# Attention over lists of neighbours: scores and values of two heads by one 128x128 weight load, with zeros beside the queries

## The chip, the cores and the metric

The kernel runs on one core of a Trainium2 chip. The time is the device time of one execution in microseconds (us). The kernel before takes 2416.37 us, the median of three timed runs (2408.73 to 2416.6). The profile is of a further execution, which took 2205.58 us. A core has five engines with queues of their own: TensorE (PE; its weight loads are shown as PEld), VectorE (DVE), ScalarE (ACT), GpSimd (POOL) and SyncE (SP), which here only issues transfers. TensorE writes into PSUM; the other data lie in SBUF, with 128 partitions each.

## The reference

One layer for 4096 tokens of width 512: attention with a mask, and then a mixture of 8 experts of which each token uses 2.

```python
adj = jnp.maximum(adjacency_matrix, eye)
q = jnp.einsum('nd,hdk->hnk', node_matrix, Wqs)        # 8 heads of 64
k = jnp.einsum('nd,hdk->hnk', node_matrix, Wks)
v = jnp.einsum('nd,hdk->hnk', node_matrix, Wvs)
scores = jnp.einsum('hqk,hmk->hqm', q, k) * kd ** (-0.5)
scores = scores + IDENTITY_BIAS * eye - MASK_VAL * (1.0 - adj)
att = jax.nn.softmax(scores, axis=-1)
return jnp.einsum('hqm,hmk,hko->qo', att, v, Wo)
...
x = x + attention(layernorm(x), adj)
x = x + experts(layernorm(x))      # top 2 of 8, exact gelu, hidden width 512
```

All is in float32. The adjacency is random and thin: most pairs of tokens are masked.

## The kernel before

The kernel has three stages. In the first it normalizes, projects queries, keys and values, writes them to DRAM and finds, for each block of 128 queries, the list of keys that any of its queries sees. In the second it does the attention over these lists. In the third it runs the experts. The change touches only the second stage.

The work of that stage is a row of items. A block of 128 queries has one item for its own 128 keys (the diagonal, `c = -1`) and one for each 128 keys of its list, `LISTED` of them, 363 in all. A list is sorted so that its first items hold keys that only the first 64 queries see and its last ones keys that only the last 64 see; such a half item is computed for 64 queries, the others for 128. By the constants, 134 of the 363 are for 128 queries, beside the 32 diagonal ones.

```python
FIRST_ALONE = [10, 6, 5, 5, 4, ...]      # items of the first half alone
SECOND_FROM = [25, 14, 12, 10, 10, ...]  # from here, of the second half alone
...
def load_q(i):                            # P = 128, NP = 4 pairs of heads, KD = 64
    q_in[i] = qp.tile([P, NP, P], F32, tag="q", name=f"q_{i}")
    nc.sync.dma_start(out=q_in[i], in_=qT_d[:, :, ts(i, P)])
```

For each item the keys and values are gathered by GpSimd, nine items ahead. Then TensorE turns the keys around, multiplies keys by queries, and multiplies values by the exponentials, all with the two heads of a pair in two halves of the array:

```python
def turn(n):
    kT[n] = work.tile([P, NP, P], F32, tag="kT", bufs=3, ...)
    pk = ps_k.tile([P, 2, TB], F32, tag="k", ...)
    for p in range(NP):
        for r in range(2):
            half = slice(r * KD, (r + 1) * KD)
            nc.tensor.transpose(pk[:, r, ts(p, KD)], kv[n][half, ts(p, P)], ident[half, half])
    nc.scalar.copy(kT[n].rearrange(...), pk[...].rearrange(...))

def scores(n):
    ...
    for p in range(NP):
        for r in range(2):
            rows = slice(r * KD, (r + 1) * KD)
            nc.tensor.matmul(part(s[r], i, c)[:, p, :], k[rows, p, :], q_in[i][rows, p, q],
                             start=True, stop=True)
    ...
    for r in range(2):
        nc.scalar.activation(e[:, r * NP : (r + 1) * NP], part(s[r], i, c), AF.Exp)

def masked(n):                            # e = e * mask, on VectorE
    ...

def values(n):
    ...
    for p in range(NP):
        for r in range(2):
            h = 2 * p + r
            nc.tensor.matmul(
                po[i][r * KD : (r + 1) * KD, p, q], v[:, ts(h, KD)], e[:, r * NP + p, :],
                start=(c < 0 and p == 0), stop=(c == listed[i] - 1), ...)
    if c >= 0:
        nc.vector.tensor_add(acc[i][:, :, q], acc[i][:, :, q], e)
```

In a product the operand that comes second is the one that is loaded into the array (128 columns of keys, or 64 columns of values), and the third one streams through it, one column for each query.

The loop runs the three steps of different items side by side. After a block's last item its sums, its output projection and the gates of the experts follow in pieces, one for each later item:

```python
for n, (i, c) in enumerate(items):
    ...                                   # fetch(n + 9), load_q, load_x
    if c < 0 and i:
        osb[i - 1] = single.tile([P, NP, P], F32, tag="o", bufs=2, ...)
        nc.scalar.copy(osb[i - 1], po.pop(i - 1))
    if n + 3 < len(items):
        turn(n + 3)
    if n + 2 < len(items):
        scores(n + 2)
    values(n)
    later(n)                              # a piece of the block before
    if n + 2 < len(items):
        masked(n + 2)
```

Of the kernel before, what the change touches and what calls it, by code (L numbers as in the profile page):

```python
# [20 lines left out]
P = 128  # L21
# [22 lines left out]
def kernel(  # L44
# [172 lines left out]
    waiting = []  # L217

    def load_q(i):
        q_in[i] = qp.tile([P, NP, P], F32, tag="q", name=f"q_{i}")  # L220
        nc.sync.dma_start(out=q_in[i], in_=qT_d[:, :, ts(i, P)])

    def gather(to, src, of, i, c):

# [43 lines left out]
    with tc.tile_pool(name="wqkv", bufs=1) as wp, tc.tile_pool(name="p1", bufs=3) as work, tc.tile_pool(  # L268
# [355 lines left out]
        for u in range(8 * NTB + 1):  # L624
            b, s = divmod(u, 8)
            if u in load_at:
                load_adj(load_at[u])
            due = []
            for k in range(8):
                if u - k in lists_from:  # L630
                    due += lists_at(lists_from[u - k], k)
            nxt = (b + 1) * TPB
            if b < NTB:
                if b + 1 < NTB:
                    if s < 4:
                        tokens_1(nxt + s)
                    else:
                        tokens_2(nxt + s - 4)
                        if b + 2 < NTB:
                            load_x1(nxt + TPB + s - 4)  # L640
                if s < 4:
                    project_kv(b, s)
                else:
                    if s == 4:
                        qT = block.tile([P, NP, TB], F32, tag="qT", name=f"qT_{b}")
                    project_q(b, s - 4, qT)
                    if s == 7:
                        nc.sync.dma_start(out=qT_d[:, :, ts(b, TB)], in_=qT)
                if b + 1 < NTB and s >= 4:
                    tokens_3(nxt + s - 4)  # L650
            if u - 2 in load_at:
                neighbours(load_at[u - 2])
                if load_at[u - 2] == NT - 1:

                    ap_cm.__exit__(None, None, None)
                    kv_cm = tc.tile_pool(name="kv", bufs=AHEAD + 1, side="right")
                    kvp = kv_cm.__enter__()
                    q_cm = tc.tile_pool(name="q", bufs=2, side="right")
                    qp = q_cm.__enter__()
                    load_q(0)  # L660
                    fetch(0)
            if u == 8 * NTB - 4:
                for n in range(1, AHEAD):
                    fetch(n)
            for f in due:
                f()
            if u - 8 in lists_from:
                g = lists_from[u - 8]
                ready += [
                    (i, c) for i in range(g * G, g * G + G) for c in range(listed[i])  # L670
                    if c % 5 in (1, 3)
                ]
            if u < 8 * NTB - 4:
                for _ in range(min(3, len(ready))):
                    pack()
# [26 lines left out]
    def route_1(m, l, pool, name):  # L702


        own = l.unsqueeze(3).to_broadcast([P, m, E, E])
        other = l.unsqueeze(2).to_broadcast([P, m, E, E])
        ahead = pool.tile([P, m, E, E], F32, tag="ahead", name=f"ahead_{name}")
        nc.vector.tensor_tensor(ahead, other, own, op=ALU.is_gt)
        same = pool.tile([P, m, E, E], F32, tag="same", name=f"same_{name}")
        nc.vector.tensor_tensor(same, other, own, op=ALU.is_equal)  # L710
        nc.vector.tensor_mul(same, same, before.unsqueeze(1).to_broadcast([P, m, E, E]))
        nc.vector.tensor_add(ahead, ahead, same)
        rank = pool.tile([P, m, E], F32, tag="rank", name=f"rank_{name}")
        nc.vector.tensor_reduce(rank, ahead, axis=AX.X, op=ALU.add)
        chosen = pool.tile([P, m, E], BF16, tag="chosen", name=f"chosen_{name}")
        nc.vector.tensor_single_scalar(chosen, rank, 2.0, op=ALU.is_lt)
        counts = pool.tile([P, m, E], BF16, tag="counts", name=f"counts_{name}")
        nc.vector.tensor_copy(counts, count.unsqueeze(1).to_broadcast([P, m, E]))
        if m > 1:
            more = pool.tile([P, E], F32, tag="chosen_m", name=f"chosen_m_{name}")  # L720
            nc.vector.tensor_reduce(
                more, chosen.rearrange("p m e -> p e m"), axis=AX.X, op=ALU.add
            )
            nc.vector.tensor_add(count, count, more)
        else:
            nc.vector.tensor_add(count, count, chosen[:, 0])
        return rank, chosen, counts
# [115 lines left out]
    with tc.tile_pool(name="p2a", bufs=2) as two, tc.tile_pool(  # L843
# [36 lines left out]
                group_of[i] = len(groups) - 1  # L880

        def load_x(i):
            x_in[i] = two.tile([P, D], F32, tag="xt", name=f"xr_{i}")
            nc.sync.dma_start(out=x_in[i], in_=x[ts(i, P), :])

        def turn(n):
            kT[n] = work.tile([P, NP, P], F32, tag="kT", bufs=3, name=f"kT_{n}")

            pk = ps_k.tile([P, 2, TB], F32, tag="k", name=f"pk_{n}")
            for p in range(NP):  # L890
                for r in range(2):
                    half = slice(r * KD, (r + 1) * KD)
                    nc.tensor.transpose(  # L893
                        pk[:, r, ts(p, KD)], kv[n][half, ts(p, P)], ident[half, half]
                    )
            nc.scalar.copy(  # L896
                kT[n].rearrange("k p (r j) -> k r p j", r=2),
                pk[:, :, : NP * KD].rearrange("k r (p j) -> k r p j", p=NP),
            )

        def queries(i, c):
            h = half_of(i, c)
            return slice(0, P) if h is None else ts(h, QH)

        def part(t, i, c):

            if half_of(i, c) is None:
                return t
            heads = t.shape[1]
            t = t.rearrange("p h q -> p (h q)")[:, : heads * QH]  # L910
            return t.rearrange("p (h q) -> p h q", h=heads)

        def scores(n):

            i, c = items[n]
            s = [ps_s.tile([P, NP, P], F32, tag="s", name=f"s{r}_{i}_{c}") for r in range(2)]
            k = kT.pop(n)
            q = queries(i, c)
            for p in range(NP):
                for r in range(2):  # L920
                    rows = slice(r * KD, (r + 1) * KD)
                    nc.tensor.matmul(  # L922
                        part(s[r], i, c)[:, p, :], k[rows, p, :], q_in[i][rows, p, q],
                        start=True, stop=True,
                    )
            if c < 0:
                e = two.tile([P, 2 * NP, P], F32, tag="acc", name=f"acc_{i}")
                acc[i] = e
            else:
                e = part(work.tile([P, 2 * NP, P], F32, tag="e", name=f"e_{i}_{c}"), i, c)  # L930
            for r in range(2):
                nc.scalar.activation(e[:, r * NP : (r + 1) * NP], part(s[r], i, c), AF.Exp)  # L932
            es[n] = e

        def masked(n):
# [7 lines left out]
        def values(n):  # L943
            i, c = items[n]
            e = es.pop(n)
            if c < 0:
                po[i] = ps_o.tile([P, NP, P], F32, tag="o", name=f"po_{i}")
            v = kv.pop(n)[:, H * KD :]
            q = queries(i, c)
            for p in range(NP):  # L950
                for r in range(2):
                    h = 2 * p + r

                    nc.tensor.matmul(  # L954
                        po[i][r * KD : (r + 1) * KD, p, q], v[:, ts(h, KD)], e[:, r * NP + p, :],
                        start=(c < 0 and p == 0), stop=(c == listed[i] - 1),
                        skip_group_check=True,
                    )
            if c >= 0:
                nc.vector.tensor_add(acc[i][:, :, q], acc[i][:, :, q], e)  # L960

# [3 lines left out]
        LAST = 6  # L965
        jobs = []
        first_of_step = []

        def piece(i, k):
            g = group_of[i]  # L970
# [2 lines left out]
            if k == 1:  # L973
                sums[i] = ps_e.tile([P, P], F32, tag="e", name=f"sums_{i}")
                a = acc.pop(i)
                for t in range(2):
                    for q in range(4):
                        u, r = divmod(q, 2)
                        nc.tensor.matmul(
                            sums[i][q * Q4 : (q + 1) * Q4], half_q[:, t],  # L980
                            a[:, r * NP + 2 * u + t, :], start=(t == 0), stop=(t == 1),
                            tile_position=(0, q * Q4), skip_group_check=True,
                        )
            if k == 2:
# [119 lines left out]
        for n, (i, c) in enumerate(items):  # L1104
# [2 lines left out]
                fetch(n + AHEAD)  # L1107
            if c == 2 and i + 1 < NT:
                load_q(i + 1)
            if c == 2:  # L1110
                load_x(i)
            if n >= 56 and n % 7 == 0 and loads:
                e, d = loads.pop(0)
                nc.sync.dma_start(out=w1[:, e, d], in_=W1[e, ts(d, P), :])
            if c < 0 and i:
                osb[i - 1] = single.tile([P, NP, P], F32, tag="o", bufs=2, name=f"o_{i - 1}")
                nc.scalar.copy(osb[i - 1], po.pop(i - 1))
            if n + 3 < len(items):
                turn(n + 3)
            if n + 2 < len(items):  # L1120
# [4 lines left out]
                masked(n + 2)  # L1125
            if c == listed[i] - 1:
                left.append((n, i))
        osb[NT - 1] = single.tile([P, NP, P], F32, tag="o", bufs=2, name=f"o_{NT - 1}")
        nc.scalar.copy(osb[NT - 1], po.pop(NT - 1))

        work_cm.__exit__(None, None, None)
        q_cm.__exit__(None, None, None)
# [286 lines left out]
```

## Time and profile before

| | us |
|---|---|
| timed, median of 3 | 2416.37 |
| profiled execution | 2205.58 |
| span of its trace | 2203.7 |
| attention stage, about | 510 to 1590 |
| experts, about | 1630 to 2190 |

The costliest groups of the page that belong to the stage of the change follow. A row names line, engine, operation, output and inputs, the shape in the array (rows*columns) and of the tile, and the count; after the first bar stand the busy time and the mean of one in ns, after the second the idle time of the engine before them and what ended it. In TensorE's groups the mean is longer than the busy time divided by the count, as instructions overlap.

```profile
L922 PE MATMUL s<-q,kT 64*128 64x64 f32 (+1 forms) x5808 | 409.4, 282 | 2.7 <-ACT acc L932 2.7
L922 PEld LDWEIGHTS s<-q,kT 64*128 64x128 f32 x5808 | 373.4, 196 | 2.9 <-ACT acc L932 2.9
L954 PE MATMUL po<-e,kv 128*64 128x64 f32 (+1 forms) x5808 | 311.3, 251 | 0.0
L954 PEld LDWEIGHTS po<-e,kv 128*64 128x64 f32 x5808 | 246.4, 141 | 34.7 <-issue 0.8
L893 PE MATMUL pk<-ident,kv 64*128 64x64 f32 x2904 | 172.4, 240 | 11.4 <-ACT kT L896 11.0
```

L893 is the transpose of the keys, L922 the scores, L954 the values. The 5808 of L922 are 363 listed items by 8 products by 2 instructions; a float32 product is two instructions, a transpose is one. The diagonal items stand in smaller groups of their own.

### The profile page before, as it was taken

Reading aid. Unit: us, or ns where it says so; the run is one execution under the profiler, and the core shown is the slowest. Engines: PE = TensorE matmul, PEld = TensorE weight load, DVE = VectorE, ACT = ScalarE, POOL = GpSimd, SP = SyncE. Lnnn points to the kernel's source line nnn. Section 1 sums busy time; section 2 is a strip of 40 time slices with the busy share of each in tenths; the row PEclk is TensorE's granted clock in tenths of the full one; section 3 lists DMA queues with packets and bytes.
Section 4 is the critical chain, followed back from the end, with each engine's and each line's share of the span. In section 5 each row is a group of like instructions: output and inputs, shape, how many; then the busy total and the mean of one; then the engine's idle time right before and its main releaser. Section 6 shows DMA issues by size and latency. Waiting matters only on the chain. (4 is left out here: it accounts for less than half of the span.)

```text
span 2203.7 us, 52479 instructions
## 1 busy us (share of the span) xinstructions
PE 2040.5 (93%) x20620; PEld 1366.7 (62%) x20620; DVE 1319.2 (60%) x2387; ACT 870.1 (39%) x1842; POOL 1242.8 (56%) x1072
## 2 busy tenths in 40 slices
PE   7877879899999999999999999999829999999998
PEld 3333334348888888888788878777614444444444
DVE  4888586724887767777677777777723222333232
ACT  2121211124666646655556555656412222222222
POOL 1769888885888657678676766667412112111112
PEclk9988988896999989999999999999959999999999
DMA  7737787847788868878788878878475556555554
GB/s 281 301 127 234 258 294 261 263 120 236 247 260 273 273 216 275 281 239 282 247 268 266 267 249 248 264 234 252 165 257 127 134 131 136 136 134 140 137 136 96
DMA packets 215039, 481.71 MB, mean 219 GB/s; under 512 B 49618, under 2 KB 81874, under 8 KB 210692
## 3 DMA queue, kind: packets, MB, share of 16 engines
q0 software_dynamic: 79232, 242.18, 37.1%
q1 hardware_dynamic: 134404, 234.01, 33.7%
q8 instruction: 168, 2.75, 0.5%
q10 hardware_dynamic: 1152, 2.10, 0.3%
q14 instruction: 83, 0.68, 0.1%
HBM read 400.59 MB, written 77.58 MB: 217 GB/s over the span
## 5 line engine op out<-in xcount | busy, mean ns | idle before, releaser
L225 POOL DMA_INDIRECT kv<-kv_d,key_of x363 | 430.4, 1186 | 231.8 <-PE po L954 136.4
L941 DVE TENSOR_TENSOR e<-e,mask 128x512 f32<-128x512 f32 (+1 forms) x363 | 322.6, 889 | 204.0 <-ACT e L932 200.4
L922 PE MATMUL s<-q,kT 64*128 64x64 f32 (+1 forms) x5808 | 409.4, 282 | 2.7 <-ACT acc L932 2.7
L1354 POOL DMA_INDIRECT out_dram<-y,r x71 | 110.6, 1558 | 474.0 <-ACT h L1324 124.7
L922 PEld LDWEIGHTS s<-q,kT 64*128 64x128 f32 x5808 | 373.4, 196 | 2.9 <-ACT acc L932 2.9
L896 ACT COPY kT<-pk 128x512 f32<-128x512 f32 x395 | 232.1, 588 | 285.1 <-PE pk L893 277.3
L932 ACT ACTIVATE e<-s 128x256 f32<-128x256 f32 (+1 forms) x726 | 297.1, 461 | 101.5 <-PE s L922 98.6
L960 DVE TENSOR_TENSOR acc<-acc,e 128x512 f32<-128x512 f32 (+1 forms) x363 | 320.4, 883 | 1.4 <-PE po L954 1.4
L954 PE MATMUL po<-e,kv 128*64 128x64 f32 (+1 forms) x5808 | 311.3, 251 | 0.0
L225 POOL DMA_INDIRECT mask<-in_adjT_dram,mask_of x230 | 257.7, 1121 | 71.9 <-issue 50.0
L457 POOL TENSOR_SCALAR started<-slots,base 128x384 bf16<-128x384 int16 (+12 forms) x96 | 229.0, 2401 | 76.6 <-DVE longer L407 75.7
L954 PEld LDWEIGHTS po<-e,kv 128*64 128x64 f32 x5808 | 246.4, 141 | 34.7 <-issue 0.8
L1318 PE MATMUL ph<-w,xT 128*128 x568 | 258.3, 598 | 0.7 <-ACT xT L207 0.7
L1347 PE MATMUL py<-w,hT 128*128 x568 | 255.6, 593 | 0.9 <-DVE hT L1332 0.9
L352 DVE TENSOR_REDUCE flags<-adjT 128x64 f32<-128x4096 f32 x32 | 141.2, 4413 | 81.2 <-DMA adjT<-in_adjT_dram 81.2
L1352 DVE TENSOR_TENSOR y<-py,bb 128x512 f32<-128x512 f32 x71 | 49.1, 692 | 225.6 <-PE py L1347 184.2
L893 PE MATMUL pk<-ident,kv 64*128 64x64 f32 x2904 | 172.4, 240 | 11.4 <-ACT kT L896 11.0
L893 PEld LDWEIGHTS pk<-ident,kv 64*128 64x128 f32 x2904 | 122.0, 142 | 77.0 <-issue 47.2
L1318 PEld LDWEIGHTS ph<-w,xT 128*128 128x128 f32 x568 | 103.2, 192 | 104.1 <-issue 103.0
L1347 PEld LDWEIGHTS py<-w,hT 128*128 128x128 f32 x568 | 102.5, 190 | 104.0 <-issue 102.8
L225 POOL DMA_INDIRECT pm<-in_adjT_dram,mask_of x133 | 130.5, 981 | 41.5 <-issue 33.6
L1353 ACT ACTIVATE y<-y,gate 128x512 f32<-128x512 f32 x71 | 51.2, 722 | 213.1 <-DVE y L1352 213.1
(589 smaller groups left out, 2405.3 us busy)
## 6 DMA issues: line engine op xcount, KB each, us to landing
adjT<-in_adjT_dram SPq DMA_DIRECT2D x32, 2048.0 KB
bb<-in_L_ffn_b_dram SPq DMA_DIRECT2D x142, 256.0 KB
r<-xs_d SPq DMA_DIRECT2D x71, 258.0 KB
kv_d<-kv SPq DMA_DIRECT2D x32, 512.0 KB
xt<-in_x_dram SPq DMA_DIRECT2D x32, 256.0 KB
qT_d<-qT SPq DMA_DIRECT2D x8, 1024.0 KB
q<-qT_d SPq DMA_DIRECT2D x32, 256.0 KB
xr<-in_x_dram SPq DMA_DIRECT2D x32, 256.0 KB
```

What stands on the lines that cost most here:

```text
L225: nc.gpsimd.indirect_dma_start(out=to, out_offset=None, in_=src, in_offset=bass.IndirectOffsetOnAxis(ap=of[:, at[i] + c : at[i] + c + 1], ...
L352: nc.vector.tensor_reduce(flags[g][:, :, j, :], adj_in.pop(i).rearrange("p c (h q) -> p h c q", h=2), axis=AX.X, op=ALU.max,)
L457: nc.gpsimd.tensor_scalar(started[i, k], slots[:, t0 * P : t1 * P], base[g][:, k, j : j + 1], None, op0=ALU.is_ge,)
L893: nc.tensor.transpose(pk[:, r, ts(p, KD)], kv[n][half, ts(p, P)], ident[half, half])
L896: nc.scalar.copy(kT[n].rearrange("k p (r j) -> k r p j", r=2), pk[:, :, : NP * KD].rearrange("k r (p j) -> k r p j", p=NP),)
L922: nc.tensor.matmul(part(s[r], i, c)[:, p, :], k[rows, p, :], q_in[i][rows, p, q], start=True, stop=True,)
L932: nc.scalar.activation(e[:, r * NP : (r + 1) * NP], part(s[r], i, c), AF.Exp)
L941: nc.vector.tensor_mul(e, e, m.unsqueeze(1).to_broadcast(e.shape))
L954: nc.tensor.matmul(po[i][r * KD : (r + 1) * KD, p, q], v[:, ts(h, KD)], e[:, r * NP + p, :], start=(c < 0 and p == 0), stop=(c == listed[i ...
L960: nc.vector.tensor_add(acc[i][:, :, q], acc[i][:, :, q], e)
L1318: nc.tensor.matmul(ph, xTs[b][:, c, :], w1[:, bass.ds(es[b], 1), c, :], start=(c == 0), stop=(c == DC - 1),)
L1347: nc.tensor.matmul(py, hTs[b][:, c, :], w2[:, bass.ds(es[b], 1), c, :], start=(c == 0), stop=(c == HC - 1),)
```

## The change

The two heads of a pair are no longer put into two halves of the array. One load of 128 x 128 holds the keys (or the values) of both heads. For the scores, the queries of the two heads stand side by side, 256 columns in place of 128, and each has zeros in the rows of the other head, so that a column of the product holds the scores of one head alone. For the values both heads' exponentials stream through both heads' values; of the product's four quarters the two with a head's own values are kept, and the other two are left in PSUM unused. The aim is one weight load where there were two, and no products in parts of the array.

```diff
     def load_q(i):
-        q_in[i] = qp.tile([P, NP, P], F32, tag="q", name=f"q_{i}")
-        nc.sync.dma_start(out=q_in[i], in_=qT_d[:, :, ts(i, P)])
+        q_in[i] = q_two[i % 2]
+        for r in range(2):
+            rows = slice(r * KD, (r + 1) * KD)
+            nc.sync.dma_start(out=q_in[i][rows, :, r, :], in_=qT_d[rows, :, ts(i, P)])
...
+                    q_two = [qp.tile([P, NP, 2, P], F32, name=f"q_{k}") for k in range(2)]
+                    for t in q_two:
+                        for r in range(2):
+                            rows = slice(r * KD, (r + 1) * KD)
+                            nc.gpsimd.memset(t[rows, :, 1 - r, :], 0.0)
...
         def turn(n):
-            pk = ps_k.tile([P, 2, TB], F32, tag="k", name=f"pk_{n}")
+            pk = ps_k.tile([P, NP, P], F32, tag="k", name=f"pk_{n}")
             for p in range(NP):
-                for r in range(2):
-                    half = slice(r * KD, (r + 1) * KD)
-                    nc.tensor.transpose(
-                        pk[:, r, ts(p, KD)], kv[n][half, ts(p, P)], ident[half, half]
-                    )
-            nc.scalar.copy(kT[n].rearrange(...), pk[...].rearrange(...))
+                nc.tensor.transpose(pk[:, p, :], kv[n][:, ts(p, P)], ident)
+            nc.scalar.copy(kT[n], pk)
...
         def scores(n):
-            s = [ps_s.tile([P, NP, P], F32, tag="s", name=f"s{r}_{i}_{c}") for r in range(2)]
             for p in range(NP):
-                for r in range(2):
-                    rows = slice(r * KD, (r + 1) * KD)
-                    nc.tensor.matmul(
-                        part(s[r], i, c)[:, p, :], k[rows, p, :], q_in[i][rows, p, q],
-                        start=True, stop=True,
-                    )
+                if p == 0 or full and p == NP // 2:
+                    s.append(ps_s.tile(
+                        [P, NP // 2, 2, P] if full else [P, NP, 2, QH], F32, tag="s",
+                        name=f"s{p}_{i}_{c}",
+                    ))
+                nc.tensor.matmul(
+                    s[-1][:, p - (len(s) - 1) * NP // 2], k[:, p, :], q_in[i][:, p, :, q],
+                    start=True, stop=True,
+                )
...
-            for r in range(2):
-                nc.scalar.activation(e[:, r * NP : (r + 1) * NP], part(s[r], i, c), AF.Exp)
+            m = H // len(s)
+            for j, t in enumerate(s):
+                nc.scalar.activation(
+                    e[:, j * m : (j + 1) * m], t.rearrange("p a r q -> p (a r) q"), AF.Exp
+                )
...
         def values(n):
             if c < 0:
-                po[i] = ps_o.tile([P, NP, P], F32, tag="o", name=f"po_{i}")
+                po[i] = [
+                    ps_o.tile([P, NP // 2, 2, P], F32, tag=f"o{j}", name=f"po{j}_{i}")
+                    for j in range(2)
+                ]
...
             for p in range(NP):
-                for r in range(2):
-                    h = 2 * p + r
-                    nc.tensor.matmul(
-                        po[i][r * KD : (r + 1) * KD, p, q], v[:, ts(h, KD)], e[:, r * NP + p, :],
-                        start=(c < 0 and p == 0), stop=(c == listed[i] - 1),
-                        skip_group_check=True,
-                    )
+                j, t = divmod(p, NP // 2)
+                nc.tensor.matmul(
+                    po[i][j][:, t, :, q], v[:, ts(p, P)], e[:, 2 * p : 2 * p + 2, :],
+                    start=(c < 0 and t == 0), stop=(c == listed[i] - 1),
+                    skip_group_check=True,
+                )
...
+        def take(i):
+            osb[i] = single.tile([P, NP, P], F32, tag="o", name=f"o_{i}")
+            for j, t in enumerate(po.pop(i)):
+                for r in range(2):
+                    rows = slice(r * KD, (r + 1) * KD)
+                    nc.scalar.copy(osb[i][rows, ts(j, NP // 2), :], t[rows, :, r, :])
...
-                osb[i - 1] = single.tile([P, NP, P], F32, tag="o", bufs=2, name=f"o_{i - 1}")
-                nc.scalar.copy(osb[i - 1], po.pop(i - 1))
+                take(i - 1)
```

The wider queries need room in SBUF, so some buffers go from two to one: the copied values of a block (above), two scratch tiles of the gates' ranking, and the block's rows of x, which are now loaded at the block's eighth listed item (or its last one, if it has fewer) in place of its third. The sums of the exponentials read the heads in their new order; the work is the same.

```diff
-        ahead = pool.tile([P, m, E, E], F32, tag="ahead", name=f"ahead_{name}")
+        ahead = pool.tile([P, m, E, E], F32, tag="ahead", bufs=1, name=f"ahead_{name}")
...
-            if c == 2:
+            if c == min(7, listed[i] - 1):
                 load_x(i)
```

## The prediction

> **What bounds the kernel now.** I read the page's shares by engine first, then its 40 slices, then the table of stretches, and then TensorE's own timeline in the middle of the attention stage, because the change touches only that stage.
>
> The first is one row of the page: busy time and number of instructions of each engine. The second are two rows of the page's slices, TensorE's busy tenths and its granted clock.
>
> ```profile
> PE 2040.5 (93%) x20620; PEld 1366.7 (62%) x20620; DVE 1319.2 (60%) x2387; ACT 870.1 (39%) x1842; POOL 1242.8 (56%) x1072
> ...
> PE   7877879899999999999999999999829999999998
> ...
> PEclk9988988896999989999999999999959999999999
> ```
>
> One slice is 55 us. TensorE (PE) is at 9 from about 500 us on. The attention over the lists of neighbours lies from about 510 to 1590 us; the experts come after it. The table of stretches for these two (busy us and count of each engine, then granted clock, DMA share, GB/s):
>
> ```profile
> 510.00:1590.00 1080.00, 1059.04 (x17153) 885.92 (x17151) 795.56 (x1240) 626.00 (x1427) 742.62 (x635) 0.97 0.79 251
> 1630.00:2190.00 560.00, 549.07 (x1691) 270.54 (x1692) 165.69 (x352) 130.50 (x212) 107.54 (x69) 0.99 0.59 134
> ```
>
> In the attention stage TensorE is busy 1059 of 1080 us, 98%; VectorE 796, GpSimd 743, ScalarE 626. A busy TensorE could still hide waits inside instructions, so I looked at how the groups follow each other. TensorE's timeline at a granted clock of 1.00 (start us, length us, then line, operation, output and inputs, count):
>
> ```profile
> 1361.92 1.06 PE L922 MATMUL s<-q,kT 64*128 64x64 f32 x16
> 1362.90 1.09 PE L954 MATMUL po<-e,kv 128*64 128x128 f32 x16
> 1363.93 0.46 PE L893 MATMUL pk<-ident,kv 64*128 64x64 f32 x8
> 1364.23 1.06 PE L922 MATMUL s<-q,kT 64*128 64x64 f32 x16
> 1365.21 0.69 PE L954 MATMUL po<-e,kv 128*64 128x64 f32 x16
> 1365.83 0.46 PE L893 MATMUL pk<-ident,kv_-1_17201 64*128 64x64 f32 x8
> ```
>
> Each group starts before the one ahead of it has ended: there is no hole. So the stage is bound by TensorE, and what counts is the distance from one group's start to the next one's. From these rows and one more (scores of an item with all 128 queries, started at 1350.57, its successor at 1351.61): transposes 0.30 us; scores of 64 queries 0.98, of 128 queries 1.04; values of 64 queries 0.62, of 128 queries 1.03. The 16 instructions of a group are 8 products, each float32 product being two instructions.
>
> That scores cost nearly the same for 64 and for 128 queries says that for 64 they are held by their weight loads, not by the stream. The load rows of the same stretch:
>
> ```profile
> 1364.17 0.98 PEld L922 LDWEIGHTS s<-q,kT 64*128 64x128 f32 x16
> 1365.21 0.55 PEld L954 LDWEIGHTS po<-e,kv 128*64 128x64 f32 x16
> ```
>
> The loads of the scores fill the whole 0.98 us, two heads at a time: 8 pairs at 0.122 us.
>
> **What the Trainium skill says.** "TensorE: Matmul & The Clock Gate", Part 3 (Packing small matmuls), says that products in different row or column groups of the array run at the same time. The trace agrees: the rows of the two heads of a pair start within 0.01 us of each other, and a pair of 128 queries is done each 0.11 us. The same page, Back-to-back issue gap, gives a gap that grows in proportion to the moving columns, N/2.4 ns plus 2.5. The trace agrees in kind: an expert product of 8 instructions with 512 columns ran from 1804.07 to 1807.50 us, 0.429 us each; that is two passes of 512 columns per float32 instruction at the page's 2.4 columns a ns (427 ns). The same page, LDWEIGHTS (loading the stationary operand), says that a load costs by its columns and not by its rows, 128/1.2 = 107 ns for 128 columns. The trace shows 0.121 us for the loads of 128 rows and 128 columns of the product that spreads the inverse sums (0.97 us for 8), and the 0.122 us above for two loads of 64 rows side by side. So a full load costs no more than the pair that it replaces.
>
> **The change part by part.** Scores: 8 products of 64 rows in pairs become 4 of 128 rows. Half of the rows of the moving queries are zeros, and the heads' queries lie side by side, so the stream of each is 256 columns for a full item and 128 for a half one. The two heads streamed at the same time before; now they stream one after the other. An item has 8 instructions for scores and 8 for values, in place of 16 and 16.
>
> Full items (134 listed ones that lie in both halves, from the lists' constants, plus the 32 diagonal ones, 166): an instruction with 256 columns is half of the 0.429 us above and a little more, 0.216 us, and 8 make 1.73 us. Scores: 1.73 in place of 1.04, +0.69. Values: 1.73 in place of 1.03, +0.70. Their loads (0.12 us) hide under 0.216 us of stream.
>
> Half items (363 - 134 = 229): an instruction with 128 columns streams for 0.107 us, less than its load of 0.122, so the load sets it: 8 x 0.122 = 0.98 us, as before. The nearest thing in the trace, 8 products of 128 x 128 with 128 columns (the spread of the inverse sums), goes from 1324.82 to 1325.90, 1.08 us. I take the middle, 1.03: scores +0.05. Values: 1.03 in place of 0.62, +0.41. Here the old way gained by loading only 64 columns per head.
>
> Transposes: 8 of 64 x 64 that go four at a time become 4 of 128 x 128. In the experts' stage 4 such took from 1803.63 to 1804.07, 0.44 us, in place of 0.30: +0.14 an item.
>
> Sum at full clock: 166 x (0.69 + 0.70 + 0.14) = 254 us; 229 x (0.05 + 0.41 + 0.14) = 137 us; 391 us together. At the stage's clock of 0.97 it is 403 us.
>
> What else moves: one exp of 512 columns in place of two of 256 for half items saves ScalarE 0.66 - 0.60, some 0.06 us each on an engine that is 58% busy: nothing. The copy of a block's values out of PSUM (0.59 us) becomes four copies of 64 partitions and 256 columns, about 0.38 us each by the exp of 256 columns, 1.5 us; it stands ahead of the next block's first values, and ScalarE reaches it while TensorE does transposes and scores of about 2.2 us. I add 0.3 us for each of 32 blocks, 10 us. Queries come by two transfers in place of one with the same bytes, and the zeros are written twice at the start, ahead of need. Holding the gates' scratch tiles, the residual rows and the values' copy in one buffer each costs nothing I can see: their users are several items apart.
>
> 403 + 10 = 413 us. About 21 us of TensorE's idle time in the stage may be taken up by longer products; I take off half, 10. So +400 us in the profiled execution, and 2416 + 403 + 16, about 2835 us in the timed ones: these take 2416 where the profiled execution took 2205.58, and I add 16 us (4% of the cost) for the part of that 9.6% which is TensorE's clock and would stretch the new time as well. Nothing in the profile tells how much that is.
>
> **The rivals.** First: the halves of the array are what hurts in the timed executions, and full products run them at a better clock. For it: the timed runs are 211 us above the profiled one and no view explains it; TensorE's clock falls in some slices (the tenth of the row above stands at 6 tenths). Against it: in the profile the stage has a mean clock of 0.97, so it can give back 30 us there. If the whole 211 us came back, the time would be 2640; a speed-up would still be missing.
>
> Second: a change of the array's tiling between groups drains it ("TensorEngine Tiling (Array Packing)", Key Properties), and without halves the drains go. The trace shows no such loss: 8 x 0.122 us of loads are all of the 0.98 us from a group of scores to the values after it. If 0.1 us hid at each of two seams of an item all the same, 395 items would give 79 us back, and the time would be about 2755.
>
> Third: all products get slower in proportion to the timed executions' extra 9.6%, or the loads of half items cost 1.09 and not 1.03: 2416 + 1.096 x 440, about 2900.
>
> Fourth: loads bind TensorE everywhere, and half as many save time. For full items this would need a load longer than 0.216 us. The trace has none. It would bring the time below 2416, and I leave it a small chance because the timed executions are not explained.
>
> **Range and chances.** The mechanism, twice the streaming in a stage that is bound by streaming, is nearly certain; the size hangs on the half items and on the unexplained gap. 8 in 10: 2680 to 2930 us. Faster by over 2%: 0.05; within 2%: 0.03; slower: 0.92.
>
> **What would show it.** In the profile after: attention from about 510 to about 1990 us with TensorE busy above 97%; scores and values of full items at 1.7 us each from start to start, of half items near 1.0; transposes 0.44; no new wait of TensorE for the copies out of PSUM above 1 us each; the experts' stage unchanged at 560 us. Wrong would be: full items near 1.0 us for 8 instructions, half items' loads above 1.2 us, or a clock that differs from 0.97 by over 0.05.

## The result and the profile after

The changed kernel takes 2520.97 us, the median of four runs (2519.64 to 2522.4), beside 2416.48 us of the kernel before (2408.73 to 2420.38): a ratio of 1.0437, with a 95% interval of 1.041 to 1.0463. It is slower, by 104 us. The prediction had 2835 us and 2680 to 2930.

The same rows of the page as were shown of before (busy time and count of each engine; TensorE's busy tenths and its granted clock in 40 slices of 63 us):

```profile
PE 2333.3 (93%) x12720; PEld 1664.4 (66%) x12720; DVE 1326.9 (53%) x2387; ACT 895.4 (36%) x1709; POOL 1232.9 (49%) x1076
...
PE   7688878989999999999999999999993999999998
...
PEclk9889998999999999999999999999997999999999
```

The table of stretches of the changed kernel, attention and experts:

```profile
510.00:1895.00 1385.00, 1352.94 (x9261) 1183.43 (x9262) 803.43 (x1243) 650.92 (x1294) 733.01 (x636) 0.99 0.65 195
1940.00:2505.00 565.00, 550.55 (x1700) 271.55 (x1701) 167.62 (x356) 131.08 (x213) 107.47 (x69) 0.99 0.61 134
```

The attention stage has about half of TensorE's instructions (9261 in place of 17153) and takes 1385 us in place of 1080. The experts are unchanged. TensorE's timeline in the stage (start us, length us):

```profile
1568.36 1.06 PE L1007 MATMUL rb<-rinv,spread 128*128 128x128 f32 x8
1569.25 0.60 PE L900 MATMUL pk<-ident,kv 128*128 128x128 f32 x4
1569.69 1.89 PE L920 MATMUL s<-q,kT 128*128 128x256 f32 x8
1571.42 1.89 PE L961 MATMUL po<-e,kv 128*128 128x256 f32 x8
1573.14 0.60 PE L900 MATMUL pk<-ident,kv 128*128 128x128 f32 x4
1573.58 1.06 PE L920 MATMUL s<-q,kT 128*128 128x128 f32 x8
1574.47 1.89 PE L961 MATMUL po<-e,kv 128*128 128x256 f32 x8
1576.20 3.60 PE L1016 MATMUL py<-wo,o 128*128 128x512 f32 x8
1579.64 0.60 PE L900 MATMUL pk<-ident,kv 128*128 128x128 f32 x4
```

Read from start to start: transposes 0.44 us, scores and values of 128 queries 1.73 us each, of 64 queries 0.89 us. Against the profile of before, TensorE pays for the longer stream: a full item's scores had taken 1.04 us. So the profiled execution went from 2203.7 to 2518.5 us, by 315 us. But the timed executions went from 2416 to 2521, by 104. The profile of before was of an execution 211 us shorter than the timed ones, and the experiments had to find out what these have more.

### The profile page after: what moved, and what is told of

Its sections match the earlier page's. It is cut to its first block, busy times and chain, and to the rows that moved or that the text cites. A ratio compares the mean times of both kernels' runs of the same rounds, so it can differ in the third digit from the quotient of the medians.

```text
span 2518.5 us, 36642 instructions
## 1 busy us (share of the span) xinstructions
PE 2333.3 (93%) x12720; PEld 1664.4 (66%) x12720; DVE 1326.9 (53%) x2387; ACT 895.4 (36%) x1709; POOL 1232.9 (49%) x1076
## 5 line engine op out<-in xcount | busy, mean ns | idle before, releaser
L228 POOL DMA_INDIRECT kv<-kv_d,key_of x363 | 445.7, 1228 | 547.1 <-PE po L961 376.0
L920 PE MATMUL s<-q,kT 128*128 128x128 f32 (+1 forms) x2904 | 498.0, 315 | 4.9 <-issue 4.9
L961 PE MATMUL po<-e,kv 128*128 128x128 f32 (+1 forms) x2904 | 495.6, 313 | 0.3 <-issue 0.3
L961 PEld LDWEIGHTS po<-e,kv 128*128 128x128 f32 x2904 | 429.1, 191 | 30.1 <-issue 0.7
L920 PEld LDWEIGHTS s<-q,kT 128*128 128x128 f32 x2904 | 417.9, 192 | 26.2 <-issue 5.1
L934 ACT ACTIVATE e<-s 128x512 f32<-128x512 f32 x497 | 296.1, 599 | 147.7 <-PE s L920 85.4
L228 POOL DMA_INDIRECT mask<-in_adjT_dram,mask_of x230 | 234.3, 1019 | 73.8 <-issue 68.3
L900 PE MATMUL pk<-ident,kv 128*128 128x128 f32 x1452 | 224.7, 277 | 16.5 <-ACT kT L901 10.0
L900 PEld LDWEIGHTS pk<-ident,kv 128*128 128x128 f32 x1452 | 170.2, 142 | 57.2 <-issue 36.5
L595 PE MATMUL pq<-xT,wq 128*128 128x512 f32 x256 | 135.0, 679 | 0.0
```

The lines of the kernel that those rows point to most:

```text
L228: nc.gpsimd.indirect_dma_start(out=to, out_offset=None, in_=src, in_offset=bass.IndirectOffsetOnAxis(ap=of[:, at[i] + c : at[i] + c + 1], ...
L900: nc.tensor.transpose(pk[:, p, :], kv[n][:, ts(p, P)], ident)
L920: nc.tensor.matmul(s[-1][:, p - (len(s) - 1) * NP // 2], k[:, p, :], q_in[i][:, p, :, q], start=True, stop=True,)
L934: nc.scalar.activation(e[:, j * m : (j + 1) * m], t.rearrange("p a r q -> p (a r) q"), AF.Exp)
L961: nc.tensor.matmul(po[i][j][:, t, :, q], v[:, ts(p, P)], e[:, 2 * p : 2 * p + 2, :], start=(c < 0 and t == 0), stop=(c == listed[i] - 1), ...
```

## The experiments

The runs fell on five chips, and the kernel before was timed on each beside them. On two of these it takes 2201 to 2202 us, on three 2403 to 2416 us. A table of all runs, each with the kernel before on the same chip:

| run | us | before, us | ratio (95% interval) |
|---|---|---|---|
| e1 before again | 2420.01 | 2416.06 | 1.0014 (0.9994 to 1.0034) |
| e2 whole transposes | 2414.26 | 2416.06 | 1.0001 (0.9979 to 1.0022) |
| e3 whole transposes and scores | 2429.54 | 2416.06 | 1.0072 (1.0053 to 1.009) |
| e4 whole transposes and values | 2530.44 | 2416.06 | 1.0473 (1.0413 to 1.0532) |
| e5 split products | 2504.14 | 2201.13 | 1.1391 (1.1315 to 1.1466) |
| e6 two turn banks | 2302.79 | 2201.13 | 1.0496 (1.041 to 1.0582) |
| e7 four score banks | 2308.1 | 2201.13 | 1.0508 (1.0436 to 1.058) |
| e8 one item further | 2212.48 | 2201.13 | 1.0058 (1.004 to 1.0076) |
| e9 values together | 2585.64 | 2403.24 | 1.0695 (1.0606 to 1.0784) |
| e10 the change | 2507.45 | 2403.24 | 1.0412 (1.0369 to 1.0456) |
| e11 as e8 | 2393.73 | 2403.24 | 0.9955 (0.9936 to 0.9973) |
| e12 as e6 | 2396.46 | 2403.24 | 0.9981 (0.9954 to 1.0007) |
| e13 as e5 | 2538.83 | 2415.41 | 1.0503 (1.0446 to 1.056) |
| e14 half the gathers | 2390.52 | 2415.41 | 0.9894 (0.9863 to 0.9925) |
| e15 as e7 | 2403.07 | 2415.41 | 0.9944 (0.9924 to 0.9965) |
| e16 the change | 2488.16 | 2201.76 | 1.1308 (1.1256 to 1.1361) |
| e17 as e9 | 2229.27 | 2201.76 | 1.0141 (1.0091 to 1.019) |

**e1: the kernel before, once more, with the clock of its timed runs.** No edit.

> The kernel before once more, for the granted clock of its timed executions. Theory A (products in halves of the array are granted a lower clock in many executions, and the profiled one escaped it): timed about 2416 us at a mean clock near 0.87, against 0.949 in the profile of 2204 us. Rival B (something else than TensorE, a transfer or the start, is longer in the timed executions): timed about 2416 us at a clock near 0.95. Rival C (the chip of the first runs was at fault): about 2205 us.

Timed 2420 us, at a mean clock of 0.910 to 0.924 in all of its 20 runs. The profile is of the same length this time. Its row in the table of stretches:

```profile
510.00:1800.00 1290.00, 1205.42 (x17082) 995.29 (x17083) 794.43 (x1225) 622.41 (x1427) 726.18 (x633) 0.89 0.68 209
```

The same program has 1290 us of attention where the first profile had 1080, at a clock of 0.89 in place of 0.97, with TensorE idle for 85 us in place of 21. Theory A has the direction right and the clock too low (0.87 expected): the clock is a part of it. What happens is seen in a stretch that ends with the clock falling. First TensorE's timeline of e1, then ScalarE's:

```profile
1115.24 1.06 PE L922 MATMUL s<-q,kT 64*128 64x64 f32 x16
1116.23 0.71 PE L954 MATMUL po<-e,kv 128*64 128x64 f32 x16
1117.37 0.40 PE L893 MATMUL pk<-ident,kv_-1_11503 64*128 64x64 f32 x5 [0.44 <-ACT kT L896]
1118.16 0.29 PE L893 MATMUL pk<-ident,kv_-1_11503 64*128 64x64 f32 x3 [0.39 <-issue]
1118.29 0.38 PE L922 MATMUL s<-q,kT 64*128 64x64 f32 x2
1119.40 2.10 PE L922 MATMUL s<-q,kT 64*128 64x64 f32 x14 [0.73 <-ACT e L932]
```

```profile
1116.73 0.58 ACT L896 COPY kT<-pk 128x512 f32<-128x512 f32 x1 [2.05 <-PE s L922]
1118.96 0.66 ACT L932 ACTIVATE e<-s 128x256 f32<-128x256 f32 x2 [1.64 <-PE pk L893]
```

The scores are recorded as done at 1116.30, yet ScalarE's exps of them start at 1118.96; it idled for 1.64 us before. In the first profile exps follow their scores at once; these end at 1319.06:

```profile
1318.00 1.06 PE L922 MATMUL s<-q,kT 64*128 64x64 f32 x16
1319.09 0.66 ACT L932 ACTIVATE e<-s 128x256 f32<-128x256 f32 x2
```

In e1 the tiles come free late, TensorE waits for PSUM (0.73 us at the second tile of the next scores), and then 14 instructions take 2.10 us where 16 take 1.06: the granted clock goes from 1.00 to 0.50 at 1119.40. The Trainium skill, "TensorE: Matmul & The Clock Gate", Part 1, puts the fall to half speed after an idle window of about 3.4 us. This trace agrees that idle time goes ahead of the fall, but not that it takes so long a pause: in the 3.4 us before it TensorE idled for about 1.6 us in three pieces, and before the stage's 32 falls for 0.1 to 3.1 us, 1.2 in the median.

I took this lateness from all traces: of each wait of ScalarE, VectorE or GpSimd that a TensorE signal ended (a signal is the semaphore by which one engine tells another that it has done), the time from that instruction's recorded end to the signal. In the attention stage of e1 it is 0.24 us in the mean, and over 0.2 us in 35% of some 900 waits; in the first profile 0.03 us and 0%. In the experts' stage it is 0.014 us in both. Signals from ScalarE to TensorE come within 0.012 us in both. So the lateness is of TensorE. The ends of TensorE's instructions are modelled in these profiles, so the record doesn't tell a signal that comes late from a product that itself ends late. Of the 214 us that the stage of e1 is longer (1304 against 1090 from the first score to the last value), TensorE's idle time is 64, the clock (some 185 us more of busy time at half speed) about 92, and the rest, about 58, is in groups drawn out.

**e2, e3, e4: one part of the change at a time.** All three are the changed kernel with parts back in halves. e2 has scores and values in halves, so that only the transposes are whole; in e3 also the scores are whole, in e4 also the values.

```diff
 # e2 and e4: the scores in halves
-    nc.tensor.matmul(s[-1][...], k[:, p, :], q_in[i][:, p, :, q], start=True, stop=True)
+    for r in range(2):
+        rows = slice(r * KD, (r + 1) * KD)
+        nc.tensor.matmul(s[r][:, p, :], k[rows, p, :], q_in[i][rows, p, r, q],
+                         start=True, stop=True)
 # e2 and e3: the values in halves
-    nc.tensor.matmul(po[i][j][:, t, :, q], v[:, ts(p, P)], e[:, 2 * p : 2 * p + 2, :], ...)
+    for r in range(2):
+        h = 2 * p + r
+        nc.tensor.matmul(po[i][r * KD : (r + 1) * KD, p, q], v[:, ts(h, KD)], e[:, h, :], ...)
```

> The changed kernel with scores and values back in halves, so only the transposes (and the smaller buffers) are the new ones. By the profiled rate, 395 items by 0.14 us more than before: span near 2259 us in an execution at a clock of 0.95. Theory A: timed some 200 us above that, near 2470. Rival that the transposes in halves are what costs clock: timed near 2260.

> The changed kernel with the values alone back in halves. Scores whole cost 166 x 0.69 - 229 x 0.09 = 94 us over e2 at full clock: about 2353. If the halves of the scores cost the clock (theory A, scores), timed equals that; if the halves of the values do, timed is about 200 us above, 2550.

> The changed kernel with the scores alone back in halves. Values whole cost 166 x 0.70 + 229 x 0.27 = 178 us over e2 at full clock: about 2437. If the halves of the scores cost the clock, timed is some 100 to 200 us above, 2540 to 2640; if those of the values do, timed is 2437.

2414, 2430 and 2530 us. e2 costs nothing over the kernel before, though TensorE has more to do in it: so on this chip TensorE's own work isn't what sets 2416 us. e3 lies between its two expectations (2353 and 2550); e4 comes close to the lower end of what guilty scores were to give (2540), but late signals don't go by one kind of half: 24% of them are over 0.2 us late in e3, 20% in e4, 31% in e2, 13 to 15% in the changed kernel (e10 and the profile after). Beside 35% in e1, that falls with each part that is made whole. The time doesn't fall with it, as whole products give TensorE more work.

The traces also show what I had left out of these sums. TensorE's timeline of the first profile, then of e2:

```profile
1357.99 3.70 PE L1001 MATMUL py<-wo,o 128*128 128x512 f32 x8
1361.62 0.46 PE L893 MATMUL pk<-ident,kv 64*128 64x64 f32 x8
```

```profile
1366.86 3.70 PE L1009 MATMUL py<-wo,o 128*128 128x512 f32 x8
1370.40 0.60 PE L900 MATMUL pk<-ident,kv 128*128 128x128 f32 x4
1370.93 1.11 PE L919 MATMUL s<-q,kT 64*128 64x64 f32 x16
```

The output projection (py) has the same shape in all kernels. From start to start it goes for 3.63 us between groups in halves (before), 3.54 when whole transposes follow (e2), and 3.44 between whole groups (after). The spread of the inverse sums (rb) goes for 1.08 us before and 0.89 after. That is 0.1 us for each seam, a change of the array's tiling between two groups, which the Trainium skill calls a drain ("TensorEngine Tiling (Array Packing)", Key Properties) without a figure.

**e5 and e13: more instructions, no halves.** The changed kernel with each product of 256 columns as two of 128.

```diff
-    nc.tensor.matmul(s[-1][..., p, :, :], k[:, p, :], q_in[i][:, p, :, q], ...)
+    for r in [slice(0, 1), slice(1, 2)]:          # full items; the values likewise
+        nc.tensor.matmul(s[-1][..., p, r, :], k[:, p, :], q_in[i][:, p, r, q], ...)
```

> The changed kernel with every product of 256 columns cut into two of 128 columns with the same 128x128 load: no tiling of the array, but 166 x 16 more product instructions and as many more loads, so nearly as many TensorE instructions in the stage as e3. Theory M (what the halves cost beyond their streams is the change of tiling, some 0.1 us at each seam, and waits for other engines): loads set the pace at 0.111 us, 166 x 2 x 0.05 = 17 us more than the changed kernel, about 2538. Rival N (TensorE's instruction count is what costs, some 13 us per thousand products with their loads, from the excess of the kernel before and of e2 to e4): 35 us more than that, 2575.

> e5 once more, for a chip on which the kernel before takes about 2410 us and TensorE's signals come late. Theory P (the signals come late the more instructions TensorE runs in a time, whether or not they are in halves of the array): share of signals over 0.2 us late as in e3 and e4, 20 to 25%, and a time of the changed kernel's 2507 to 2521 plus 17 plus waits, 2540 to 2570. Rival Q (they come late because of products in halves): 14% as in the changed kernel, or less, and 2525 to 2538. On a chip where the kernel before takes 2201 us: 2504 as e5 measured.

e5 fell on a chip where the kernel before takes 2201 us; it took 2504, with no signal over 0.2 us late. e13 fell on one where it takes 2415: 2539, 16% late. The changed kernel takes 2488 on the one kind and 2507 to 2521 on the other, so the split costs 16 us on the first and 18 to 32 on the second, where 17 were worked out. The count of instructions alone isn't what makes signals late (theory P had 20 to 25%): e13 has 11906 of TensorE's in the stage with 16% late, e3 12380 with 24%, and the changed kernel about 9300 with 13 to 15%. The time doesn't decide: 2539 is just under P's 2540 and just over Q's 2538.

The traces show one thing more: how often a signal is late goes with how short the product is that sends it, whole ones too. In the two traces of the changed kernel on such chips (the profile after, e10) 20% of the signals are late after whole products of 128 streamed columns (1127 waits), 7% after 256 (737), none after 512 (64); in e13, which cuts the 256, it is 17% after all of 128. In the first stage, with whole products in all kernels, 33% of 151 are late after products of 35 columns, over the twelve traces with late signals. In the experts' stage none of 2510 is late, though 846 follow transposes of 128 columns: those stand between products of 512. So short products in close order fit what is seen, and halves, two to each 0.11 us, are an extreme of it; no run tells the two apart.

**e6, e7, e8: more room between the engines.** e6 is e2 with two PSUM buffers for the transposes, e7 is e2 with four for the scores, e8 is the kernel before with its scores one item further ahead.

```diff
 # e6
-    name="ps_k", bufs=1, space=PSUM
+    name="ps_k", bufs=2, space=PSUM
 # e7
-    name="ps_s", bufs=3, space=PSUM
+    name="ps_s", bufs=4, space=PSUM
 # e8
-    turn(n + 3); scores(n + 2); values(n); later(n); masked(n + 2)
+    turn(n + 4); scores(n + 3); values(n); later(n); masked(n + 3)
```

> e2 (whole transposes, scores and values in halves) with two PSUM buffers for the transposes in place of one, so that TensorE doesn't wait when ScalarE copies them late. Theory H (the kernel before is held in its timed executions by late handoffs from TensorE to ScalarE, and TensorE's idling then lowers its clock): faster than e2's 2414, by 20 to 70 us. Rival (TensorE itself is slower in halves, whatever the buffers): 2414.

> e2 with four PSUM buffers for the scores in place of three, so that an item's second tile need not wait for the exps of the item before. Theory H: faster than e2's 2414, by 20 to 70 us; more than e6 if the waits inside the groups of scores are the larger part, as the trace of e1 suggests. Rival (TensorE itself is slower in halves): 2414.

> The kernel before with transposes, scores and masks one item further ahead of the values (and one more buffer of exponentials; the room for it comes from the same small buffers as in the change). Theory H: VectorE's and ScalarE's lateness has one item, some 2.7 us, more to hide in: faster than 2416 by 30 us or more. Rival (TensorE itself is slower in halves, or the waits are for PSUM buffers, which are the same three and two): 2416.

These landed on the chip with 2201 us, where there is no lateness to hide, so they don't test theory H; they show TensorE as the bound there. 2303 and 2308 are whole transposes in place of halves: 102 and 107 us by 395 items, 0.26 to 0.27 us each, and not the 0.14 of the whole kernel, as a whole transpose between halves ends in a seam (0.58 us from start to start in e2).

The same kernels on chips where signals come late:

> e8 once more. Where the kernel before takes 2416 us, theory H expects at least 30 us less, as one more item stands between scores and values; its rival (the transposes' and scores' own PSUM buffers are what TensorE waits for) expects no change. Where it takes 2201 us, 2212 as e8 measured.

> e6 once more. Where the kernel before takes 2416 us, theory H expects less than e2's 2414 by 20 to 70 us; a TensorE that is itself slower expects 2414. Where it takes 2201 us, 2303 as e6 measured.

> e7 once more. Where the kernel before takes 2410 us: the trace of e1 has its stalls inside the groups of scores just ahead of the second tile, which waits for the exps of the item before; with a fourth buffer these go. Theory H: at least 20 us less than e2 and e12, about 2380. Rival (TensorE's own lateness is the cause and the buffer wait its symptom): 2400 to 2414. On a chip where the kernel before takes 2201 us: 2308.

2394 beside 2403, 2396 beside 2403 and 2403 beside 2415. e8's further item brings 0.5%, the fourth buffer 0.6%, the second one for the transposes nothing sure. Theory H in the form I gave it, that more room for the handoffs gives 20 to 70 us back, falls. This fits waits for buffers that are a symptom of TensorE's lateness: removing one of them doesn't remove it.

**e14: half the gathers left out.** Every second listed item works on the keys and values of the item before it, so the output is that of other keys.

```diff
-    kv[n] = kvp.tile([P, KV], F32, tag="kv", ...)
+    again = c > 0 and c % 2 == 1
+    kv[n] = kv[n - 1] if again else kvp.tile([P, KV], F32, tag="kv", ...)
 ...
-    gather(kv[n], kv_d, key_of, i, c)
+    if not again:
+        gather(kv[n], kv_d, key_of, i, c)
```

> The kernel before, but every second listed item takes the keys and values of the item before it in place of a gather of its own: half of the gathers are left out, and the values computed are those of other keys. TensorE's work is unchanged. Theory R (transfers beside TensorE make its signals late; the experts' stage, with 134 GB/s in place of 200 to 260, shows none late): where the kernel before takes 2410 us, well under 2350 and few late signals. Theory P: still about 2400. Where the kernel before takes 2201 us: about the same 2201, as TensorE sets the pace there.

```profile
560.00:1700.00 1140.00, 1072.59 (x15610) 883.08 (x15610) 724.39 (x1110) 566.85 (x1302) 511.69 (x424) 0.91 0.49 147
```

2391 beside 2415 us, and 24% late signals in place of 35%, at 147 GB/s in place of 209 (e1). The gathers have a share in the lateness; they are not the cause of most of it (theory R had well under 2350). GpSimd, which issues the gathers, has less to do as well, and e14 doesn't tell the two apart.

**e9 and e17: the values of two items side by side.** The values of every second item come ahead of a step's transposes and scores, with so much less time for their masks. Transposes and scores have the same tiling in the rows (64*128), so an item of the kernel before has two seams, at both ends of its values, and this edit takes two in four away, not one in six as I had expected.

```diff
+    if n % 2:
+        values(n)
     turn(n + 3); scores(n + 2)
-    values(n)
+    if n % 2 == 0:
+        values(n)
```

> The kernel before with the values of every second item issued ahead of that step's transposes and scores, so that the values of two items stand side by side. Theory M (each change of the array's tiling costs TensorE about 0.1 us): one seam in six goes, 0.05 us an item, 395 x 0.05 = 20 us less where the kernel before takes some 2201 us, about 2181. Rival (no cost at the seams): no change. Where the kernel before takes 2416 us, TensorE doesn't set the pace alone, and either reads less.

> e9 once more. Where the signals are prompt, theory M (a seam between tilings costs 0.1 us) expects 20 us less than the kernel before, 2181, less what the earlier values wait for their masks; its rival 2201. Where they are late: 2585 as e9 measured.

Slower in both: by 28 us (1.4%) where signals are prompt, by 182 where they are late. TensorE's timeline of e17:

```profile
1404.59 1.06 PE L922 MATMUL s<-q,kT 64*128 64x64 f32 x16
1405.49 0.46 PE L893 MATMUL pk<-ident,kv 64*128 64x64 f32 x8
1405.79 1.43 PE L922 MATMUL s<-q,kT 64*128 64x64 f32 x16
1407.15 0.69 PE L954 MATMUL po<-e,kv 128*64 128x64 f32 x16
```

Scores that are followed by transposes go for 0.90 us and not 0.98 as when values follow, and two groups of values side by side of 64 queries go for 1.08 us in the median where two alone go for 1.24: the seams are there, and by these two numbers the edit should have saved 0.24 us for two items, some 47 us and not 20. But the scores now follow each other so closely that the second waits for its PSUM tiles (1.36 us), in about a third of the groups. The saving was given back, and e17 doesn't measure it at the end. What e9 shows is how little room the kernel before has: some 1.3 us less (a step's transposes and scores) for half of the items costs 182 us where signals come late.

**e10 and e16: the change on both kinds of chip.**

> The changed kernel beside the kernel before on this chip. Theory H (the kernel before is bound by TensorE where the handoffs are prompt, and by late handoffs where its trace shows them; the changed kernel is bound by TensorE in both): about 2490 to 2520 us whichever the chip; the ratio is 1.13 where the kernel before takes 2201 us, 1.04 where it takes 2416. Rival (the chip is slower in all): the ratio is the same 1.04 on both.

> The changed kernel once more. Where TensorE's signals are prompt and the kernel before takes 2201 us: TensorE's work alone gives 2201 + 166 x 1.39 + 395 x 0.14 + 229 x (0.27 - 0.09) - 22 for the pieces of the gates and the output projection, about 2490, a ratio of 1.13. Where they are late: 2507 to 2521, a ratio of 1.04.

2507 us beside 2403 (1.041), and 2488 beside 2202 (1.131). The table of stretches of e16:

```profile
510.00:1870.00 1360.00, 1350.76 (x9305) 1187.33 (x9305) 808.82 (x1262) 663.46 (x1298) 744.87 (x638) 0.99 0.67 199
```

TensorE is busy 99.3% of the stage. The expected sum, worked through, comes to 2506 and not to the 2490 written beside it; measured 2488. It leaves out, among others, the clock: in the first profile 70 us of TensorE's busy time in the stage ran at half speed, in e16 14, which gives some 28 us back. So where signals are prompt the change costs 286 us, with TensorE busy all the while. The changed kernel loses 19 to 33 us where signals come late, the kernel before 201 to 214.

## Why the prediction was right or wrong

- **The bound and the direction: right.** TensorE bounds the stage in the profile shown, twice the streaming is slower, and the time is 4.4% up.
- **Full items: right.** 1.73 us each for scores and values, 0.44 for transposes, as worked out.
- **Half items: mis-sized.** The term was 1.03 us for 8 instructions of 128 columns; measured 0.89. An instruction goes for 0.111 us, not 0.122: what I read as loads filling the whole 0.98 us was 8 x 0.11 and a seam of 0.1, and the 1.08 us of the spread, the other end of my middle, held two seams. 229 x 2 x 0.14 = 64 us too much.
- **The second rival, the drains: wrongly put aside, by the same misreading.** Seams cost 0.1 us. Most of their saving was already in the start-to-start distances I took from before; beyond these, the unchanged pieces of a block got shorter (the output projection and the spread by 0.19 us each, the gates' transposes and logits by 0.15 to 0.18), some 22 us in all, which I had left out. Against that stand new seams around the sums and the gates' product, whose tiling (128*32) is unchanged: values of 128 queries ahead of the sums take 1.82 us in e16 where they take 1.73 otherwise, which makes an estimated 9 us with the others.
- **The clock: 0.99 in the stage in place of 0.97.** Most of the 12 us added for it was not due. With these and the copies below, the predicted +400 of the profiled execution becomes about +300; measured +286 between timed runs with prompt signals (e16), +315 between the two profiles, of which the second has late signals.
- **The step that failed: adding it all to 2416.** I took the 211 us between the profile and the timed runs as a part that stays, and even stretched it by 16 us. It is no TensorE work at all, but waits on late signals, a lower clock and groups drawn out (64, 92 and about 58 us in e1's stage), and the changed kernel loses little of that on the same kind of chip: its stage in the profile after is 31 us longer than in e16, of which 23 is idle time and none the clock. So 286 us of new work less some 182 that are no longer lost make 104. The first rival said that the 211 us could come back and gave 2640 (2835 less 211 is 2624); most of it did come back, with the half items on top. Its reason, the halves themselves, is not shown. The profile of before, by itself, doesn't show the loss; the table of times beside it did, with 2416 against 2205.58, and I took that as a remark and not as a second bound. None of my signs of being wrong came (full items 1.73 us, half items' instructions 0.89, clock 0.99): all of them watched the profile, and the failure lay outside it.
- **Copies of the values: the size right, the cost not.** They take 0.37 us each, as estimated. TensorE waited 11.4 us for them in 11 blocks (after) and 5.4 us in 2 (e16), but it had waited 6.3 us in 2 blocks before: 5 us more at most, where 10 were added.
- **What stays open:** why TensorE's signals come late on some chips. It isn't its count of instructions alone (e13), and it isn't the gathers alone (e14); kernels with scores and values in halves have more of it (31 to 35% against 13 to 15%), but whole products have it too, the shorter the more. Each chip was used in one stretch of time, so chip and time aren't told apart either, and on which chip the first profile was taken isn't on record; its signals are prompt, as on the chips with 2201 us.

## What to carry to other kernels

Zeros that fill up an array in place of two half products doubled the stream here and saved only seams and loads: 1.73 us in place of 1.04 for 128 queries; for 64 queries 0.89 in place of 0.98 for scores, where the stream had not set the pace, but 0.89 in place of 0.62 for values. Before adding a cost to a time, ask whether that time is the profile's: here the timed runs were 10% above it, with a second bound, and some 182 of 286 us of new work on the first one were free. The kernel before has little to spare at its handoffs (e9), and takes 2201 us on one chip and 2416 on another: compare kernels on the same chip.

## What the runs showed of the hardware

- TensorE's signals to other engines came 0.014 to 0.033 us in the mean after the recorded end on two chips and in the first profile; with the same program on one of the three others 0.24 us in the mean, over 0.2 us in 35% of the waits (e1). Other kernels on the three had 13 to 35% late. In e1 the recorded clock was full at 272 of 311 late ones. Whether the signal or the product itself is late, the record doesn't tell.
- On those chips 20% of the signals were late after whole products of 128 columns, 7% after 256, 0% after 512 (e10 and the profile after).
- A change of the array's tiling costs about 0.1 us (3.63, 3.54, 3.44 us for one and the same group with two, one and no such seam). Scores and transposes, both 64*128 in the array, follow each other without one (0.90 us for 8 pairs at 0.11, e17).
- A 128x128 float32 load with 128 streamed columns goes for 0.111 us an instruction (the profile after); two loads of 64 rows side by side under 64 columns go for the same 0.11 (e17), where 64 of the 512 columns that take 0.429 us would be 0.054, so there it isn't the stream.
